# A four-layer graph network: the attention rows stay in two PSUM banks, and the other six are split anew

## The chip, the cores and the metric

The kernel runs on one core of a Trainium2 chip. The metric is the device time in microseconds of one execution. The figure before is the median of three executions. Everything is float32. The profile of one more execution gives the start and length of every instruction on the engines: TensorE (PE; its weight loads are PEld), VectorE (DVE), ScalarE (ACT) and GpSimd (POOL).

## The reference, cut to what matters

Input x holds 128 graphs of 128 nodes with 512 features; adj is one 128x128 matrix. Four layers follow each other, each with a residual and a layer norm:

```python
def layer0(x):  return einsum('bnd,do->bno', einsum('nm,bmd->bnd', adj, x), weight) + bias
def layer1(x):                                   # scores without softmax, normed by row
    q, k, v = x @ Wq.T, x @ Wk.T, x @ Wv.T
    rel = adj.T * einsum('bnd,bmd->bnm', q, k)
    return einsum('bnm,bmd->bnd', rel / norm(rel, axis=2, keepdims=True), v)
def layer2(x):                                   # attention from two dot products per node
    h = x @ W
    s1, s2 = h @ a[:512, 0], h @ a[512:, 0]
    e = leaky_relu(s1[:, :, None] + s2[:, None, :], 0.2) * adj
    return elu(einsum('bij,bjf->bif', softmax(e, axis=2), h) + beta * h)
def layer3(x):                                   # C - A is the bias: both use adj
    A = einsum('od,bdn->bon', adj, x); C = A + b
    return max(relu(A[:, :, None, :] + (C - A)[:, :, :, None]), axis=-1)
for layer in (layer0, layer1, layer2, layer3):
    x = layernorm(x + layer(x))
```

Since h = x W, the two dot products per node are x · (W a1) and x · (W a2): two rows of 512 numbers that are the same for every node and graph. The kernel computes them once and calls them wa.

## The kernel before

Graphs go in 32 groups of four. Work is emitted in pieces, each with a place in a table; all pieces are sorted by place, and every engine runs its own in that order. A group is spread over some 110 places and a new one begins every 28, so pieces of several groups stand among each other. The three dense products with 512x512 weights, and the q-k product with a merged matrix m_qk, are done by seven block products in place of eight (a Strassen scheme), in three PSUM regions r0, r1 and r2.

```python
psum = tile_pool(name="psum", bufs=4, space=PSUM)        # 4 buffers of each tag
def bank(name):                                          # one bank of 128 x 512 fp32
    return psum.tile([P, D], FP, tag="ps", name=name)
...
wa = const.tile([P, 2, D], FP)                           # SBUF
...
def prepare_rows():                                      # once
    for i in range(2):
        p = bank(f"p_wa{i}")
        for k in range(K):                               # K = 4
            pe.transpose(p[:, k * P : (k + 1) * P],
                         col[:, i, k : k + 1].to_broadcast([P, P]), ident)
        act.copy(wa[:, i, :], p)
    dve.tensor_reduce(wa_sum, wa, AX.X, ALU.add, negate=True)
...
ORDER = (1, 2, 6, 5, 7, 3, 4)                            # of the seven products
REGION = {1: 0, 6: 0, 7: 0, 4: 0, 2: 1, 5: 2, 3: 2}      # the region each adds to
def product(at, name, mul, s, w, c, fresh, begin=None):
    def step(i):
        where = REGION[i]
        first = i in (1, 2, 5)
        if first:
            r[where] = psum.tile([P, 2, H], FP, tag="r", name=f"r{where}_{name}")
        mul(r[where], s["f"][i], bw[w][i], first)        # 4 matmuls of 256 columns
    def out(i):                                          # the region as it stands, to a block
        p, dst = r[REGION[i]], c(*BLOCK[i])
        if fresh and i in (1, 6, 5, 4):
            act.copy(dst, p)
        else:
            dve.tensor_tensor(dst, p, dst, ALU.add)
    for n, i in enumerate(ORDER):
        emit(at[n], step, i)
        emit(at[n] + 0.72, out, i)
```

Products are named by their use: r_y for layer 0 (added to x), r_m and r_v for layer 1 (to tT and v), r_z for layer 2 (to c). The pieces of layers 1 and 2 around the dots:

```python
def attend(b):                                           # p_o
    s["o", b] = bank(f"p_o1_{g}_{b}")
    pe.matmul(s["o", b], s["relT"]..., s["v"][:, b, :], start=True, stop=True)
def residual(b):
    dve.scalar_tensor_tensor(x2[g][:, b, :], s["o", b], s["rn"][:, b : b + 1],
                             x1[g][:, b, :], op0=ALU.mult, op1=ALU.add)
    stats(s, f"1_{g}", b, x2[g][:, b, :])                # bn_stats, bn_aggr
def dots(b):
    for i in range(2):
        scr = work.tile([P, D], FP, tag="scr", bufs=2, ...)
        dve.scalar_tensor_tensor(scr, x2[g][:, b, :], 1.0, wa[:, i, :],
                                 op0=ALU.mult, op1=ALU.mult,
                                 accum_out=s["d"][:, i, b : b + 1])
def scale_dots():                                        # three small operations on d
    ...
# norm: ve = var + eps (VectorE), rstd = ve ** -0.5 (GpSimd), then the apply (ScalarE)
def spread():                                            # p_s: d to all partitions
    ... pe.transpose(...)
def direct(b):                                           # last group only, in place of r_z
    s["c", b] = psum.tile([P, D], FP, tag="r", name=f"c_{g}_{b}")
    for k in range(K):
        pe.matmul(s["c", b], s["zT"][:, k, ...], w2_sb[:, k, :], start=(k == 0), stop=(k == K - 1))
def elu(b):                                              # x<-c,x and x<-m,x
    dve.scalar_tensor_tensor(x, s["c", b], 0.0, x2[g][:, b, :], op0=ALU.max, op1=ALU.add)
    dve.scalar_tensor_tensor(x, s["m", b], 1.0, x, op0=ALU.min, op1=ALU.add)
```

GpSimd meanwhile adds the bias of layer 0 (x<-x,bias_sb) and forms the sums that the block products need (s_y, s_x, s_z), all from SBUF. Part of the table:

```python
residual=row(51.0, 1), dots=row(54.2, 1.1), norm1=[55.2], scale=[58.8],
```

where row(a, step) is four places, one for each graph.

Of the kernel before, what the change touches and what calls it, by code (L numbers as in the profile page):

```python
# [8 lines left out]
FP = mybir.dt.float32  # L9
# [20 lines left out]
def kernel(  # L30
# [33 lines left out]
    pe, dve, act, pool = (InOrder(tc, e) for e in (nc.tensor, nc.vector, nc.scalar, nc.gpsimd))  # L64
    sync = InOrder(tc, nc.sync)
    B, N, D = x.shape
    P = 128
# [3 lines left out]
    H = D // 2  # L71
# [4 lines left out]
    const = ctx.enter_context(tc.tile_pool(name="const", bufs=1))  # L76
    data = ctx.enter_context(tc.tile_pool(name="data", bufs=2))
    work = ctx.enter_context(tc.tile_pool(name="work", bufs=1))
    small = ctx.enter_context(tc.tile_pool(name="small", bufs=4))
    psum = ctx.enter_context(tc.tile_pool(name="psum", bufs=4, space=bass.MemoryType.PSUM))  # L80

    def bank(name):
        return psum.tile([P, D], FP, tag="ps", name=name)

    def on_all(row, n):

# [37 lines left out]
    ident = const.tile([P, P], FP)  # L124
# [3 lines left out]

    adjT = const.tile([P, P], FP)
    pt = bank("p_adjT")  # L130
    pe.transpose(pt[:, :P], adj_sb, ident)
    act.copy(adjT, pt[:, :P])
# [2 lines left out]

    m_qk = const.tile([P, K, D], FP)
    wvT = const.tile([P, K, D], FP)
    wa = const.tile([P, 2, D], FP)
    wa_sum = const.tile([P, 2], FP)
    beta_i = const.tile([P, P], FP)  # L140
    beta_b = beta_i[:, None, :].to_broadcast([P, G, P])
# [21 lines left out]
    def prepare_qk(c):  # L163

        pm = bank(f"p_m{c}")
        for e in range(K):
            pe.matmul(
                pm,
                wq_sb[:, e, c * P : (c + 1) * P],
                wk_sb[:, e, :],  # L170
                start=(e == 0),
                stop=(e == K - 1),
            )
        act.copy(m_qk[:, c, :], pm)
        if c == K - 1:
            bw["m"] = weight_blocks(m_qk, "m")

    def prepare_v(c):
        pv = bank(f"p_wv{c}")
        for e in range(K):  # L180
            pe.transpose(pv[:, e * P : (e + 1) * P], wv_sb[:, e, c * P : (c + 1) * P], ident)
        act.copy(wvT[:, c, :], pv)
        if c == K - 1:
            bw["v"] = weight_blocks(wvT, "v")

    col = const.tile([P, 2, K], FP)
# [15 lines left out]
    def prepare_rows():  # L202

        for i in range(2):
            p = bank(f"p_wa{i}")
            for k in range(K):
                pe.transpose(
                    p[:, k * P : (k + 1) * P], col[:, i, k : k + 1].to_broadcast([P, P]), ident
                )
            act.copy(wa[:, i, :], p)  # L210
        dve.tensor_reduce(wa_sum, wa, AX.X, ALU.add, negate=True)
        dve.tensor_scalar(beta_i, ident, beta_sb, None, op0=ALU.mult)

# [6 lines left out]
    def emit(at, f, *args):  # L220
        pieces.append((at, lambda: f(*args)))
# [5 lines left out]
    def row(at, step, n=G):  # L227
        return [at + i * step for i in range(n)]
# [6 lines left out]
        move=row(20.5, 0.1), x_sums=row(25.3, 0.5), m=row(28, 1, 7), scores=row(36.5, 1),  # L235
        masked=[39.95], squares=[40.4], turn_rel=[40.3],
        move_rel=row(41.2, 0.1), inverse=[42.5], v=row(42, 1, 7), attend=row(50.6, 1),
        residual=row(51.0, 1), dots=row(54.2, 1.1), norm1=[55.2], scale=[58.8],
        apply1=row(65.4, 0.33),
        spread=[61.6], leaky=[62.0], weighted=[63.4], greatest=[64.3], exps=[64.4],  # L240
        divide=[65.8], turn_att=[68.6], with_beta=[69.0], gather=row(71.5, 1),
# [15 lines left out]
            scale=[5.6], apply1=row(24.3, 0.8), spread=[6.9], leaky=[7.4], weighted=[9.0],  # L257
# [11 lines left out]
            scale=[47.0], apply1=row(47.5, 0.8), spread=[48.9], leaky=[49.4], weighted=[51.0],  # L269
# [69 lines left out]
    def product(at, name, mul, s, w, c, fresh, begin=None):  # L339


        r = {}

        def step(i):
            if i == 1 and begin is not None:
                begin()
            where = REGION[i]
            first = i in (1, 2, 5)
            if first:
                r[where] = psum.tile([P, 2, H], FP, tag="r", name=f"r{where}_{name}")  # L350
            mul(r[where], s["f"][i], bw[w][i], first)

        def out(i):
# [9 lines that stand above are left out]
# [251 lines left out]
    def layer2(g, t):  # L614
        s = {}
# [83 lines left out]

        def direct(b):  # L700

            s["c", b] = psum.tile([P, D], FP, tag="r", name=f"c_{g}_{b}")
            for k in range(K):
                pe.matmul(
                    s["c", b],
                    s["zT"][:, k, b * P : (b + 1) * P],
                    w2_sb[:, k, :],
                    start=(k == 0),
                    stop=(k == K - 1),
                )  # L710
# [25 lines left out]
        if g < NG - 1:  # L736
            left_factors(t["z_sums"], s, "zT", "s_yz", f"z_{g}", 0)
            product(t["z_w"], f"z_{g}", by_rows, s, "2", rows_of(lambda: s["c"]), True, begin)
        else:
            each(t["z_w"], direct)  # L740
# [35 lines left out]
    each(row(18.0, 0.1), prepare_v)  # L776
    each(row(29.2, 1.8), prepare_dots)
    emit(40.7, prepare_rows)
    emit(61.0, prepare_2)
    for g in range(NG):  # L780
# [33 lines left out]
```

## Time and profile before

| | |
|---|---|
| device time, median of 3 | 2239.06 us (2235.84 to 2239.59) |
| profiled execution | 2236.61 us, of which the span from first to last instruction is 2234.4 us |
| granted TensorE clock | 0.996 of full speed in the mean |
| DMA | 115.15 MB, 52 GB/s in the mean; queues' share of the engines 20% |

In the profile's lines an instruction stands by the tile that it writes and those that it reads (out<-in), with buffer and group numbers left out: scr<-x,wa is a dot, r_m<-xT,m_qk a block product of m, tT<-r_m the addition that reads its region, x<-p_o,rn,x the residual of layer 1, p_s the spread of the dots' result d. A line "A <- B: us, times, longest" says how long in total engine and tile A waited for B. In a timeline each line is a start in us, a length in us, and the instruction (x8: eight in a row); the bracket at its end is the idle time of the engine before it and what ended it. Each float32 matmul of the program appears as two records, so that a block product of four matmuls is "x8". The chain that ended last is 75% TensorE and 20% VectorE.

### The profile page before, as it was taken

How to read it: one execution, taken by the hardware profiler on the slowest of the kernel's cores; microseconds unless marked ns; L12 is line 12 of the kernel's file. 1: busy time of each engine (PE TensorE's matmuls, PEld its weight loads, DVE VectorE, ACT ScalarE, POOL GpSimd, SP SyncE). 2: the span in 40 equal slices, each digit the busy share in tenths (PEclk: the TensorE clock that was granted, in tenths of full speed). 3: DMA queues.
4: the chain of work that ended last, by engine and by line, in shares of the span. 5: the costliest groups of instructions: out<-in, count | busy, mean ns of one | idle time of the engine just before them, and what ended most of it. 6: DMA issues, size and time to landing. Idle time of an engine off the chain costs nothing.

```text
span 2234.4 us, 31661 instructions
## 1 busy us (share of the span) xinstructions
PE 2182.9 (98%) x11073; PEld 1842.1 (82%) x11073; DVE 1794.9 (80%) x3534; ACT 980.0 (44%) x1936; POOL 983.1 (44%) x743
## 2 busy tenths in 40 slices
PE   7999999999999999999999999999999999999996
PEld 5888888888888888888888888888888888888873
DVE  4668888778878788888788888788888788887788
ACT  2224444444444454444444444444344444444535
POOL 3435454435455344544344554344553354443322
PEclk9999999999999999999999999999999999999998
DMA  4010222211222211222201222202222112221101
GB/s 166 25 32 19 60 57 62 62 28 40 60 59 62 62 19 48 59 60 62 59 19 52 58 61 62 52 22 55 57 62 63 41 28 59 58 62 43 21 28 57
DMA packets 333294, 115.15 MB, mean 52 GB/s; under 512 B 297424, under 2 KB 297552, under 8 KB 333136
## 3 DMA queue, kind: packets, MB, share of 16 engines
q1 hardware_dynamic: 331936, 110.77, 19.6%
q10 hardware_dynamic: 1200, 2.36, 0.3%
q8 instruction: 89, 1.46, 0.3%
q14 instruction: 69, 0.57, 0.1%
HBM read 39.65 MB, written 33.55 MB: 33 GB/s over the span
## 4 chain that ended last, share of the span: by engine, by line
PE 75%; DVE 20%; issue 3%; POOL 1%; ACT 1%; DMA 0%; DVEq 0%; ACTq 0%; POOLq 0%
PE r_v L26 17%; PE r_y L26 15%; PE r_z L26 14%; PE r_m L26 8%; DVE scr L26 6%; DVE x L26 6%; PE p_z L26 5%; PE p_o L26 5%; PE p_a L26 5%; PE p_rel L26 4%; DVE st L26 2%; PE p_y L26 2%; DVE tT L26 1%; DVE d L26 1%; PE p_m L26 1%
## 5 line engine op out<-in xcount | busy, mean ns | idle before, releaser
L26 ACT ACTIVATE x<-x,nmean,rstd 128x512 f32<-128x512 f32 x512 | 385.8, 808 | 187.5 <-DVE nmean L26 187.4
L26 DVE BATCH_NORM_STATS2 st<-x 128x6 f32<-128x512 f32 x512 | 352.1, 688 | 56.7 <-ACT x L26 47.9
L26 DVE SCALAR_TENSOR_TENSOR scr<-x,wa 128x512 f32<-128x512 f32 x256 | 286.2, 1169 | 0.0
L26 POOL TENSOR_TENSOR rstd<-ve,mhalf 128x4 f32<-128x4 f32 (+1 forms) x134 | 145.2, 1083 | 286.9 <-DVE ve L26 280.7
L26 POOL TENSOR_TENSOR x<-x,bias_sb 128x512 f32<-128x512 f32 x128 | 193.2, 1519 | 76.9 <-PE p_y L26 76.4
L26 POOL TENSOR_TENSOR s_x<-xT 128x512 f32<-128x512 f32 x64 | 95.8, 1497 | 256.5 <-DMA xT<-xB 237.6
L26 ACT ACTIVATE x<-x,top 128x512 f32<-128x512 f32 x128 | 92.4, 722 | 229.1 <-DVE top L26 228.8
L26 DVE TENSOR_TENSOR x<-r_y,x 128x512 f32<-128x512 f32 x224 | 151.4, 676 | 27.1 <-PE r_y L26 27.0
L26 ACT COPY c<-r_z 128x512 f32<-128x512 f32 x124 | 71.8, 579 | 221.5 <-PE r_z L26 221.5
L26 ACT COPY yT<-p_y 128x512 f32<-128x512 f32 x128 | 75.1, 587 | 206.5 <-PE p_y L26 206.5
L26 PEld LDWEIGHTS p_y<-adjT,x 128*128 128x128 f32 x1024 | 135.8, 195 | 13.1 <-ACT adjT L26 5.2
L26 DVE SCALAR_TENSOR_TENSOR x<-p_o,rn,x 128x512 f32<-128x512 f32 x128 | 95.9, 749 | 59.9 <-PE p_o L26 56.0
L26 PE MATMUL p_y<-adjT,x 128*128 128x128 f32 x1024 | 136.7, 278 | 6.4 <-ACT adjT L26 4.9
L26 PEld LDWEIGHTS p_z<-eT,x 128*128 128x128 f32 x1024 | 133.9, 192 | 8.4 <-DVE x L26 1.2
L26 DVE SCALAR_TENSOR_TENSOR x<-m,x 128x512 f32<-128x512 f32 x128 | 129.7, 1013 | 13.6 <-DVE x L26 0.9
L26 PEld LDWEIGHTS p_rel<-xT,tT 128*128 128x128 f32 x1024 | 134.1, 191 | 7.4 <-DVE tT L26 0.8
L26 POOL TENSOR_TENSOR s_z<-zT 128x512 f32<-128x512 f32 x31 | 39.3, 1267 | 224.0 <-ACT zT L26 224.0
L26 PE MATMUL p_rel<-xT,tT 128*128 128x128 f32 x1024 | 134.9, 275 | 0.6 <-DVE tT L26 0.6
L26 PE MATMUL p_z<-eT,x 128*128 128x128 f32 x1024 | 134.8, 275 | 0.4 <-DVE x L26 0.4
L26 PE MATMUL p_a<-x,adjT 128*128 128x512 f32 x256 | 131.2, 597 | 3.6 <-ACT x L26 1.9
L26 ACT COPY tT<-r_m 128x512 f32<-128x512 f32 x128 | 75.7, 591 | 132.9 <-PE r_m L26 132.9
L26 PE MATMUL p_o<-v,relT 128*128 128x512 f32 x256 | 130.3, 593 | 0.0
(119 smaller groups left out, 5008.6 us busy)
## 6 DMA issues: line engine op xcount, KB each, us to landing
out_dram<-x SPq DMA_DIRECT2D x128, 256.0 KB, 2.5
x<-in_x_dram SPq DMA_DIRECT2D x31, 1024.0 KB, 5.8
xT<-xB SPq DMA_DIRECT2D x480, 64.0 KB, 2.3
relT<-relB SPq DMA_DIRECT2D x512, 16.0 KB, 1.8
w_sb<-in_L_gnn_weight_dram ACTq DMA_DIRECT2D x1, 1024.0 KB, 5.9
x<-in_x_dram SPq DMA_DIRECT2D x4, 256.0 KB, 7.9
wq_sb<-in_L_gnn_Wq_dram SPq DMA_DIRECT2D x1, 1024.0 KB, 12.1
wk_sb<-in_L_gnn_Wk_dram SPq DMA_DIRECT2D x1, 1024.0 KB, 14.9
```

Source lines behind the costliest of these rows:

```text
L26: return lambda *args, **kw: self.tc.keep_in_program_order(op(*args, **kw))
```

## The change

Each row of wa is first transposed on TensorE into a PSUM bank, from where ScalarE copies it to SBUF. The change leaves the rows in PSUM, in a tile of two banks that lives to the end, and the dots read them there. That is meant to take one of a dot's two inputs out of SBUF. Six banks remain: the general tag "ps" has 3 in place of 4, and the tag "r" (4) becomes "r0" with 2 for region 0 and the last group's direct products, and "r12" with 1 for regions 1 and 2 together. The table moves the dots between the residuals, and norm1 and scale forward.

```diff
-    psum = ctx.enter_context(tc.tile_pool(name="psum", bufs=4, space=bass.MemoryType.PSUM))
+    psum = ctx.enter_context(tc.tile_pool(name="psum", bufs=1, space=bass.MemoryType.PSUM))
     def bank(name):
-        return psum.tile([P, D], FP, tag="ps", name=name)
+        return psum.tile([P, D], FP, tag="ps", name=name, bufs=3)
@@
-    wa = const.tile([P, 2, D], FP)
+    wa = psum.tile([P, 2, D], FP, tag="wa", name="wa")
@@ prepare_rows
         for i in range(2):
-            p = bank(f"p_wa{i}")
             for k in range(K):
                 pe.transpose(
-                    p[:, k * P : (k + 1) * P], col[:, i, k : k + 1].to_broadcast([P, P]), ident
-                )
-            act.copy(wa[:, i, :], p)
+                    wa[:, i, k * P : (k + 1) * P],
+                    col[:, i, k : k + 1].to_broadcast([P, P]),
+                    ident,
+                )
@@ TABLE
-        residual=row(51.0, 1), dots=row(54.2, 1.1), norm1=[55.2], scale=[58.8],
+        residual=row(51.0, 1), dots=[51.7, 53.8, 54.9, 55.6], norm1=[54.6], scale=[57.2],
@@ product, step
-                r[where] = psum.tile([P, 2, H], FP, tag="r", name=f"r{where}_{name}")
+                r[where] = psum.tile(
+                    [P, 2, H],
+                    FP,
+                    tag="r0" if where == 0 else "r12",
+                    name=f"r{where}_{name}",
+                    bufs=2 if where == 0 else 1,
+                )
@@ direct
-            s["c", b] = psum.tile([P, D], FP, tag="r", name=f"c_{g}_{b}")
+            s["c", b] = psum.tile([P, D], FP, tag="r0", name=f"c_{g}_{b}", bufs=2)
```

## The prediction

> **What bounds the kernel now.** I read the page's busy times first, then TensorE's own waits, then the timeline of one group (the kernel runs 32 groups of four graphs; from about 220 us to 2130 us they look alike).
>
> The page, parts 1 and 5 (busy us and share; then group, count, busy us, mean ns, idle before):
>
> ```profile
> PE 2182.9 (98%) x11073; PEld 1842.1 (82%) x11073; DVE 1794.9 (80%) x3534; ACT 980.0 (44%) x1936; POOL 983.1 (44%) x743
> ...
> L26 DVE SCALAR_TENSOR_TENSOR scr<-x,wa 128x512 f32<-128x512 f32 x256 | 286.2, 1169 | 0.0
> ...
> L26 DVE SCALAR_TENSOR_TENSOR x<-p_o,rn,x 128x512 f32<-128x512 f32 x128 | 95.9, 749 | 59.9 <-PE p_o L26 56.0
> ...
> L26 DVE SCALAR_TENSOR_TENSOR x<-m,x 128x512 f32<-128x512 f32 x128 | 129.7, 1013 | 13.6 <-DVE x L26 0.9
> ```
>
> TensorE is the bound. How much of its 2183 us is really lost I worked out from the starts of its matmuls: from one start to the next it takes 216 ns for 256 columns, 429 ns for 512, 112 ns for 128 (109 ns for a transpose) when nothing holds it. Those, summed over all 11,073, give 2161.5 us. The first starts at 3.4 us, and about 13.6 us pass after the last start at 2220.8. What the starts lose beyond this is 56.4 us: 20.8 before 220 us (loads and preparation), 19.6 from 220 to 2130, and 16.0 after 2130. So a change to VectorE can win a part of 56 us, 2.5% of the time, and never the sum of its own savings.
>
> The three operations shown have 128x512 elements each. The dots (scr<-x,wa) take 1169 ns in the mean, the residual, which has one input in PSUM, 749. The means of the first and third hide two kinds: of the single records of the dots the shortest tenth is at 679 ns and the longest tenth at 1748 to 1755, with little between; those of the residual all lie from 718 to 754.
>
> TensorE's waits (us in total, times, longest):
>
> ```profile
> PE r_m L26 <- DVE tT L26: 6.8, 5, 1.7
> ...
> PE r_y L26 <- DVE x L26: 4.4, 17, 0.4
> ...
> PE p_s L26 <- DVE d L26: 3.1, 2, 2.1
> ```
>
> All three are TensorE waiting for VectorE just behind the dots: an addition that must read a PSUM region before the next product adds to it, and the transposes of the dots' result. By the starts, the losses in front of r_y and of r_m are the 19.6 us of the steady part almost wholly: 0.6 to 1.0 us before r_y in about half of the groups, and 1.4 us before r_m in four, with some tenths before the next r_y product.
>
> One group, timeline (start, us, engine): VectorE, then GpSimd, then TensorE.
>
> ```profile
> 1050.80 0.68 DVE L26 SCALAR_TENSOR_TENSOR scr<-x,wa 128x512 f32<-128x512 f32 x1
> ...
> 1051.42 0.68 DVE L26 SCALAR_TENSOR_TENSOR scr<-x,wa 128x512 f32<-128x512 f32 x1
> ...
> 1052.03 1.74 DVE L26 SCALAR_TENSOR_TENSOR scr<-x,wa 128x512 f32<-128x512 f32 x1
> ...
> 1053.70 1.75 DVE L26 SCALAR_TENSOR_TENSOR scr<-x,wa 128x512 f32<-128x512 f32 x1
> ...
> 1055.38 0.68 DVE L26 TENSOR_TENSOR tT<-r_m,tT 128x512 f32<-128x512 f32 x1
> ```
> ```profile
> 1050.28 1.46 POOL L26 TENSOR_TENSOR rstd<-ve,mhalf 128x4 f32<-128x4 f32 x1
> 1051.72 4.86 POOL L26 TENSOR_TENSOR x<-x,bias_sb 128x512 f32<-128x512 f32 x3
> ```
> ```profile
> 1048.94 1.89 PE L26 MATMUL r_m<-xT,m_qk 128*128 128x256 f32 x8
> ...
> 1054.18 1.89 PE L26 MATMUL r_m<-s_x,m_qk 128*128 128x256 f32 x8
> ...
> 1060.25 0.60 PE L26 MATMUL p_s<-ident,d 128*128 128x128 f32 x4
> 1062.13 1.99 PE L26 MATMUL r_m<-xT,t_m 128*128 128x256 f32 x8 [1.28 <-DVE tT L26]
> 1063.96 3.62 PE L26 MATMUL r_y<-w_sb,yT 128*128 128x256 f32 x16
> ```
>
> Two dots run in 0.68 us; the two that begin while GpSimd adds the bias take 1.74 us, a GpSimd operation longer. The r_m block at 1048.94 ends at about 1050.8, but its reader, the addition at 1055.38, stands behind the dots. The lateness runs on to the bracketed stall of 1.28 us.
>
> **What the Trainium skill says.** "SBUF — State Buffer", Who interferes with whom: a VectorE instruction with two SBUF inputs contends with a GpSimd instruction that reads SBUF, and one with at most one SBUF input does not; the shared pair is an exclusive lock, so the loser waits for the whole instruction. The trace agrees: 0.68 against 1.74 us for the two-SBUF dots, never over 0.754 us for the residual with its PSUM input, whatever GpSimd does. "PSUM — Partial Sum Buffer", Specifications (TRN2): eight banks of 2 KiB per partition, and a VectorE instruction may take one tensor input from PSUM. So both broadcast rows (2 x 512 fp32) are exactly two banks, and six stay for everything else; no run yet shows what six do. "Perfetto Trace Analysis", Identifying the Most-Contended Engine: TensorE's busy share is a poor measure of its headroom. The trace agrees: busy 2182.9 us, of which 2161.5 are pitch.
>
> **The change, part by part.**
>
> *The dots read PSUM.* 256 dots lose their second SBUF input. A quiet two-SBUF dot takes 0.68, the PSUM residual 0.75; I take 0.70. VectorE saves 256 x (1.169 - 0.70) = 120 us, 3.75 us a group. GpSimd also waited for the dots (1.50 to 1.79 us for operations that take 1.27 when alone); perhaps 50 us of its 983 go. Neither sum is on the path.
>
> *The dots stand earlier.* In the built program the first pair comes after the first residual, the second after the third, and the rstd power is asked for before the last two pairs; the three small d operations come before the r_m addition. Walking one group with TensorE's starts above and 0.70 per dot: last residual's statistics at about 1046.0, the r_z addition at 1046.2 to 1046.9, four dots to 1049.7, d (rstd ready at about 1049.6) to 1050.6, then the r_m addition at 1050.9 to 1051.6, now held by TensorE itself, in place of 1055.38 to 1056.06. The later additions keep some 2 us of this. The p_s wait and both r stalls go.
>
> *Two copies of wa by ScalarE* (1.1 us, once) go. Nothing.
>
> *PSUM split anew.* Before: 4 banks for ps, 4 for the r regions and the last group's direct c. After: ps 3, r0 and c 2, r1 and r2 together 1. For each PSUM tile I took from the trace its first matmul's start less the end of the last read of the tile it will now follow. In the steady groups: ps with 3 banks keeps at least 4.2 us of slack; r0 with 2 keeps 15. The single r1/r2 bank is the tight one: r1_v, r2_v, r1_z, r2_z have 2.4 to 4.3 us, r2_y 0.8, r1_m 0.5, but r1_y -0.3 and r2_m -1.1 in the median (negative means a wait). With the old dots this would cost 1.4 us a group. But the readers behind the negative ones are those very additions behind the dots: in the walk r2_m (wanted at 1054.2) finds its bank read at 1051.6, r1_m (1048.9) at 1046.9, r1_y (about 1064.3 without the stall) at 1062 to 1063.8 even if all four ELU operations in front collide with GpSimd. So no new wait in the steady groups.
>
> Start: p_wv with 3 banks waits 2.1 us for a copy, of which the next tile's old position gives back 1.6: -0.5. In group 0 the r2_m product must wait for the r_m addition (-5.1 us with old dots; about 2.7 with new), while the 2.2 us p_s stall behind it goes: -0.5. Group 1's 2.4 us go: +2.4. Sum: +1.4.
>
> End: TensorE's waits for d and tT at 2137 and 2144 (1.1 + 0.8) go. Then p_o and p_z with 3 banks wait up to 2.9 us for residuals (about 2.0 net), and the third direct c waits 1.9 for the first one's ELU, with 2 banks. The last dots save only two collisions, 2.1 us. I put the end at +2, plus or minus 3.
>
> Sum: 19.6 (say 19.5) + 1.4 + 2 = 23 us; 2239 - 23 = 2216.
>
> **Rivals.**
> *The single r1/r2 bank becomes the new wait.* For: two negative slacks of eight, and the thin walk of r1_y. Against: both are in the shadow of the dots. If it costs 1 us a group the gain is eaten: some 2240; with 1.4 us more and the old stalls kept, 19.6 + 39, so 2278.
> *VectorE's saving comes back as other collisions.* The ELU operations (x<-m,x, 1013 ns) move under the bias additions in place of the s_y sums; for: VectorE is 80% busy and GpSimd's total shrinks little. If half of the 3.75 us a group comes back, most r_y stalls stay: 2225 to 2230.
> *The end decides.* It is bound by VectorE's chain; two banks for c and three for p_z could cost 3 us more than I count: 2221.
>
> **Range and chances.** The steady gain cannot exceed 19.6, and start and end lose at most about 5 more than counted: 2207 to 2230 should hold it 8 times in 10. A gain of 2% would be 44.8 us, four fifths of all that TensorE loses; a loss of 2% needs the first rival at its worst. So within 2% is nearly certain.
>
> **What would show it.** Dots at 0.68 to 0.75 us without a second kind; VectorE busy about 1675 us, GpSimd below 960; PE <- DVE tT and DVE d gone from TensorE's waits, r_m or r_y starts without gaps, group after group 66.8 us apart. Wrong if TensorE's loss in the steady part stays above 8 us, or if r2_m or r1_y wait for VectorE's additions in most groups; or if p_z, c and p_a lose over 5 us at the end.

## The result, and the profile after

The changed kernel takes 2219.39 us (median of four executions, 2218.65 to 2220.8); the kernel before, run beside it, 2239.21 us (2235.84 to 2239.59). The ratio is 0.9916, 95% interval 0.9898 to 0.9933: 0.8% faster. The prediction was 2216 us.

The page of the changed kernel: busy times (part 1), the chain that ended last (part 4), and three groups of part 5 (count, busy us, mean ns, idle before).

```profile
PE 2173.1 (98%) x11073; PEld 1841.6 (83%) x11073; DVE 1652.0 (74%) x3534; ACT 979.0 (44%) x1934; POOL 908.2 (41%) x743
...
PE 94%; DVE 3%; POOL 1%; ACT 1%; issue 0%; DMA 0%; ACTq 0%; DVEq 0%; POOLq 0%
...
L26 POOL TENSOR_TENSOR x<-x,bias_sb 128x512 f32<-128x512 f32 x128 | 171.2, 1340 | 137.8 <-PE p_y L26 137.2
L26 DVE SCALAR_TENSOR_TENSOR x<-m,x 128x512 f32<-128x512 f32 x128 | 114.4, 894 | 112.7 <-ACT m L26 102.4
...
L26 DVE SCALAR_TENSOR_TENSOR scr<-x,wa 128x512 f32<-128x512 f32 x256 | 161.4, 675 | 0.0
```

VectorE does 142.9 us less and GpSimd 74.9 us less, and the time falls by 20. That is what a bound of TensorE looks like: its own line stays at 98%, and the chain, which was 75% TensorE and 20% VectorE, is now 94% TensorE. The dots are down to 675 ns in the mean. GpSimd's bias additions, which stood beside them, went from 1519 to 1340 ns, and the ELU operations x<-m,x from 1013 to 894.

One steady group of the changed kernel on VectorE (start us, length us):

```profile
1042.60 0.67 DVE L26 SCALAR_TENSOR_TENSOR scr<-x,wa 128x512 f32<-128x512 f32 x1
...
1044.41 0.68 DVE L26 SCALAR_TENSOR_TENSOR scr<-x,wa 128x512 f32<-128x512 f32 x1
...
1045.02 0.94 DVE L26 SCALAR_TENSOR_TENSOR d<-mv,wa_sum,d 128x4 f32<-128x4 f32 x2
1046.07 0.17 DVE L26 TENSOR_TENSOR d<-d,rstd 128x8 f32<-128x8 f32 x1
1046.29 0.69 DVE L26 TENSOR_TENSOR tT<-r_m,tT 128x512 f32<-128x512 f32 x1
```

and on TensorE:

```profile
1049.53 1.89 PE L26 MATMUL r_m<-s_x,m_qk 128*128 128x256 f32 x8
...
1055.61 0.60 PE L26 MATMUL p_s<-ident,d 128*128 128x128 f32 x4
1056.05 1.89 PE L26 MATMUL r_m<-xT,t_m 128*128 128x256 f32 x8
```

No dot takes 1.7 us any more. The addition at 1046.29 ends at 1046.98, and the product that must follow it in the single r12 bank starts at 1049.53: 2.5 us of slack. Of the kernel before, the same addition started 1.2 us *after* the start of that product. None of the three TensorE lines has a bracket, so none waited; the r_m stall of 1.28 us that the kernel before had there is gone.

What TensorE still waits for in the changed kernel (us in total, times, longest):

```profile
PE p_a L26 <- DVE mx L26: 4.9, 2, 3.2
...
PE r_m L26 <- DVE tT L26: 4.4, 1, 4.4
...
PE p_wv L26 <- ACT wvT L26: 1.9, 1, 1.9
PE c L26 <- DVE x L26: 1.8, 1, 1.8
PE r_y L26 <- DVE tT L26: 1.5, 1, 1.5
```

Each of these happens once or twice, in the start or at the end; none belongs to a steady group.

I counted TensorE's loss beyond pitch as in the prediction, here with places in the program instead of times: *start* until the first r0 product of m in group 3, *steady* until that of group 31, *end* after it. The last column is the time from that product of group 31 to the end of the span; at the end it says more than the loss, since the chain runs through VectorE too there. A steady loss of -1.7 means none: the median pitches overstate a little. Each ratio is taken to executions of the kernel before beside that run; these had medians of 2235.8 to 2239.2 us, so that the ratios compare better than the times.

| kernel | us (median) | ratio, 95% interval | start | steady | end | us after |
|---|---|---|---|---|---|---|
| before | 2239.2 | 1 | 20.8 | 19.6 | 16.0 | 105.5 |
| the change: rows in PSUM, split, new places | 2219.4 | 0.9898 to 0.9933 | 23.8 | -1.7 | 19.6 | 106.9 |
| split alone | 2264.1 | 1.0104 to 1.0139 | 27.1 | 37.5 | 22.0 | 108.8 |
| new places alone | 2215.5 | 0.9888 to 0.9926 | 16.0 | 4.2 | 14.3 | 103.8 |
| split and new places, rows in SBUF | 2280.2 | 1.0173 to 1.0218 | 26.7 | 53.6 | 20.0 | 106.9 |
| rows in PSUM and split, old places | 2212.3 | 0.9877 to 0.991 | 17.5 | -1.7 | 18.0 | 105.3 |
| the same, free banks used at the end | 2212.3 | 0.9878 to 0.9907 | 18.4 | -1.7 | 15.9 | 105.8 |
| the change, group 0's scale later | 2211.9 | 0.9876 to 0.9906 | 17.7 | -1.7 | 18.1 | 105.4 |
| before, without the bias addition | 2206.8 | 0.9851 to 0.9884 | 12.5 | -1.7 | 15.9 | 105.3 |
| PSUM, old places, start and end mended | 2210.0 | 0.9866 to 0.9895 | 15.6 | -1.7 | 15.9 | 105.8 |
| PSUM, old places, start mended alone | 2210.4 | 0.9861 to 0.9894 | 15.5 | -1.7 | 18.5 | 105.3 |

The profiled spans differ by 2234.4 - 2217.6 = 16.8 us, and the table accounts for them: +21.3 in the steady part, -3.0 at the start, -1.4 after group 31's product. The medians differ by 3 us more because the profiled execution of before was 2.6 us quicker than its median.

### The profile page after: what moved, and what is told of

Same layout as the page of the kernel before. It is cut to its first block, busy times and chain, and to the rows that moved or that the text cites. A ratio compares the mean times of both kernels' runs of the same rounds, so it can differ in the third digit from the quotient of the medians.

```text
span 2217.6 us, 31631 instructions
## 1 busy us (share of the span) xinstructions
PE 2173.1 (98%) x11073; PEld 1841.6 (83%) x11073; DVE 1652.0 (74%) x3534; ACT 979.0 (44%) x1934; POOL 908.2 (41%) x743
## 3 DMA queue, kind: packets, MB, share of 16 engines
q10 hardware_dynamic: 1200, 2.36, 0.3%
## 4 chain that ended last, share of the span: by engine, by line
PE 94%; DVE 3%; POOL 1%; ACT 1%; issue 0%; DMA 0%; ACTq 0%; DVEq 0%; POOLq 0%
PE r_y L26 17%; PE r_m L26 17%; PE r_v L26 17%; PE r_z L26 17%; PE p_z L26 5%; PE p_rel L26 5%; PE p_y L26 5%; PE p_o L26 5%; PE p_a L26 5%; DVE st L26 1%; DVE x L26 1%; PE p_eT L26 1%; PE p_m L26 1%; PE p_s L26 1%; ACT x L26 1%; POOL x L26 1%
## 5 line engine op out<-in xcount | busy, mean ns | idle before, releaser
L26 POOL TENSOR_TENSOR rstd<-ve,mhalf 128x4 f32<-128x4 f32 (+1 forms) x134 | 132.2, 986 | 307.1 <-DVE ve L26 300.8
L26 POOL TENSOR_TENSOR x<-x,bias_sb 128x512 f32<-128x512 f32 x128 | 171.2, 1340 | 137.8 <-PE p_y L26 137.2
L26 DVE SCALAR_TENSOR_TENSOR x<-m,x 128x512 f32<-128x512 f32 x128 | 114.4, 894 | 112.7 <-ACT m L26 102.4
L26 POOL TENSOR_TENSOR s_x<-xT 128x512 f32<-128x512 f32 x64 | 82.2, 1285 | 254.2 <-DMA xT<-xB 243.3
L26 DVE SCALAR_TENSOR_TENSOR scr<-x,wa 128x512 f32<-128x512 f32 x256 | 161.4, 675 | 0.0
L26 PE MATMUL r_m<-s_x,m_qk 128*128 128x256 f32 x512 | 123.1, 384 | 4.4 <-DVE tT L26 4.4
```

The costliest lines, as they stand in the source:

```text
L26: return lambda *args, **kw: self.tc.keep_in_program_order(op(*args, **kw))
```

## The experiments

My theory after the result was that the steady stalls were the late r_m additions, that the quick dots cleared them, and that the new places mattered little. The rivals were that the split costs what the negative slacks say, and that the earlier places do the work. Rows in PSUM without the new split would need ten banks of the eight, so every version with the rows in PSUM has the split.

### The new split alone

The rows of wa stay in SBUF and the dots where they were; only the banks are divided as in the change (ps 3, r0 2, r12 1; two banks stay unused).

```diff
-    psum = ...tile_pool(name="psum", bufs=4, ...)
+    psum = ...tile_pool(name="psum", bufs=1, ...)
-        return psum.tile([P, D], FP, tag="ps", name=name)
+        return psum.tile([P, D], FP, tag="ps", name=name, bufs=3)
-                r[where] = psum.tile([P, 2, H], FP, tag="r", ...)
+                r[where] = psum.tile([P, 2, H], FP, tag="r0" if where == 0 else "r12", ...,
+                                     bufs=2 if where == 0 else 1)
-            s["c", b] = psum.tile([P, D], FP, tag="r", ...)
+            s["c", b] = psum.tile([P, D], FP, tag="r0", ..., bufs=2)
```

> The kernel before with the new PSUM split alone (rows of wa in SBUF, two banks left empty, old table). Theory A, waits overlap: a TensorE that is held at r_m is not held again at r_y, so each steady group loses about the 1.1 us of r_m in place of the 0.7 us it lost before; with some 7 us more at start and end: 2250 to 2260 us. Rival of the prediction, waits add: 1.4 us a group come on top of the old ones: 2278 us. Rival B, the split is free away from start and end: 2245 us.

Measured: 2264.1 us, ratio 1.0122 (1.0104 to 1.0139). TensorE's waits, the first line:

```profile
PE r_m L26 <- DVE tT L26: 36.2, 31, 4.8
```

Once in nearly every group; without the one of 4.8 us at the start, 1.05 us in the mean. So the negative slack of -1.1 us read from the kernel before was real and cost what it said. But the steady loss is 37.5 us, 17.9 more than before, and not 39 more: a wait for the r_m addition puts the r_y products behind it later too, so that the old stalls there vanish in it. Waits on one chain overlap; the prediction's figure of 2278 us for its first rival had added them.

### The new places alone

```diff
-        residual=row(51.0, 1), dots=row(54.2, 1.1), norm1=[55.2], scale=[58.8],
+        residual=row(51.0, 1), dots=[51.7, 53.8, 54.9, 55.6], norm1=[54.6], scale=[57.2],
```

> The kernel before with the new places of dots, norm1 and scale alone (rows in SBUF, 4 + 4 banks). Theory P, the PSUM rows are what wins: dots still collide, less than half of the steady gain: 2229 us or more. Rival T, the places alone suffice: the first two pairs of dots now run in VectorE's idle time between residuals, before GpSimd's sums begin, so the lateness behind the dots falls by some 2.3 of 4.4 us, the steady waits go (19.6 us and the negative rest), and nothing is paid at start and end: 2214 to 2219 us, as fast as the changed kernel or faster.

Measured: 2215.5 us, ratio 0.9907 (0.9888 to 0.9926), no less of a gain than the whole change, with dots that still take 1141 ns in the mean and VectorE busy for 1791.5 us. What is left of the stalls:

```profile
PE r_y L26 <- DVE x L26: 2.8, 7, 1.3
```

So a gain of this size can be had without the PSUM rows. What matters is when the additions behind the dots run, and with four banks for the regions the table alone does nearly all of that.

### Split and new places, rows in SBUF

Both edits above together, that is, the change without its PSUM rows.

> The changed kernel with the rows back in SBUF (new split, new places). Theory P: the single r1/r2 bank needs the quick dots, so r_m waits come back in most groups: 2235 to 2250 us. Rival T: the places leave about 0.4 us of slack at r_m, so steady groups stay clean and only start and end cost: 2219 to 2226 us.

Measured: 2280.2 us, ratio 1.0195 (1.0173 to 1.0218). Both expectations fell: places that help with the old banks hurt with the new ones. VectorE in one group of this kernel:

```profile
1135.84 1.77 DVE L26 SCALAR_TENSOR_TENSOR scr<-x,wa 128x512 f32<-128x512 f32 x1
...
1137.54 1.75 DVE L26 SCALAR_TENSOR_TENSOR scr<-x,wa 128x512 f32<-128x512 f32 x1
...
1139.22 1.75 DVE L26 SCALAR_TENSOR_TENSOR scr<-x,wa 128x512 f32<-128x512 f32 x1
...
1140.90 0.34 DVE L26 SCALAR_TENSOR_TENSOR d<-mv,wa_sum,d 128x4 f32<-128x4 f32 x2
1141.35 1.05 DVE L26 TENSOR_TENSOR d<-d,rstd 128x8 f32<-128x8 f32 x1
1142.32 0.68 DVE L26 TENSOR_TENSOR tT<-r_m,tT 128x512 f32<-128x512 f32 x1
```

and TensorE:

```profile
1139.93 1.05 PE L26 MATMUL p_y<-adjT,x 128*128 128x128 f32 x8
1143.05 3.44 PE L26 MATMUL r_m<-s_x,m_qk 128*128 128x256 f32 x8 [2.06 <-DVE tT L26]
```

In the new order the d operations stand ahead of the r_m addition. Three collided dots and 1.4 us of d operations are between the addition and the end of its product, and the r_m product behind it now waits 2.06 us, then runs 3.44 us instead of 1.89 (the last section returns to this). The waits of r_m for tT sum to 44.0 us in 31 times.

### Rows in PSUM and split, old places

The change without its edit of the table.

```diff
-        residual=row(51.0, 1), dots=[51.7, 53.8, 54.9, 55.6], norm1=[54.6], scale=[57.2],
+        residual=row(51.0, 1), dots=row(54.2, 1.1), norm1=[55.2], scale=[58.8],
```

> The changed kernel with the old places of dots, norm1 and scale (rows in PSUM, new split). If quick dots alone suffice, the eight dots take some 5 us in a row after the last residual, the r_m addition ends at about the same moment as in the changed kernel, and the time is the same within 3 us: 2217 to 2223 us. If places and PSUM rows each bring half, about 2229 us.

Measured: 2212.3 us, ratio 0.9894 (0.9877 to 0.991). This kernel has nothing left in its steady groups, like the change, and loses 17.5 us at the start instead of 23.8. The head of TensorE's waits:

```profile
PE p_y L26 <- ACT adjT L26: 5.1, 1, 5.1
PE p_a L26 <- DVE mx L26: 4.9, 2, 3.2
...
PE p_wv L26 <- ACT wvT L26: 1.9, 1, 1.9
PE c L26 <- DVE x L26: 1.8, 1, 1.8
PE r_y L26 <- DVE tT L26: 1.5, 1, 1.5
```

It is the list of the change but for r_m <- tT, which falls from 4.4 to 0.6 us. With quick dots the tight bank is free in time in either order, so the new places win nothing, and they cost 7.9 us by the profiled spans (5 by the ratios). The time is better than expected: I hadn't thought that these places could do harm.

### The start: group 0's scale later

The change's only long wait for an r_m addition lies at the start: by the table, group 1's product waits for an addition that stands behind group 0's d operations. On VectorE:

```profile
108.64 0.68 DVE L26 SCALAR_TENSOR_TENSOR scr<-x,wa 128x512 f32<-128x512 f32 x1
...
109.25 2.46 DVE L26 SCALAR_TENSOR_TENSOR d<-mv,wa_sum,d 128x4 f32<-128x4 f32 x2
111.81 1.12 DVE L26 TENSOR_TENSOR d<-d,rstd 128x8 f32<-128x8 f32 x1
112.86 0.68 DVE L26 TENSOR_TENSOR tT<-r_m,tT 128x512 f32<-128x512 f32 x1
```

GpSimd:

```profile
109.21 3.70 POOL L26 TENSOR_TENSOR x<-x,bias_sb 128x512 f32<-128x512 f32 x3
```

and TensorE:

```profile
108.14 1.05 PE L26 MATMUL p_y<-adjT,x 128*128 128x128 f32 x8
113.59 3.78 PE L26 MATMUL r_m<-s_x,m_qk 128*128 128x256 f32 x8 [4.39 <-DVE tT L26]
```

The three d operations, with 4 or 8 elements per partition, hold VectorE for 3.6 us in front of the addition, while GpSimd makes three bias additions of 1.2 us each. The edit gives group 0 alone a later place for them, behind the addition.

```diff
-    FIRST = {0: dict(turn=row(20.4, 0.3)), ...}
+    FIRST = {0: dict(turn=row(20.4, 0.3), scale=[58.0]), ...}
```

> The changed kernel with one place changed: group 0's three small d operations stand behind its first r_m addition. Theory D: these three, which took 1.24, 1.30 and 1.12 us beside GpSimd's bias additions, are what holds the r2_m product 4.6 us at the start; that wait falls to about 1 us and the time to 2214 to 2217 us. Rival: group 0 is late by the dots between its residuals and the third ps bank; the wait stays above 3 us and the time at 2218 to 2220 us.

Measured: 2211.9 us, ratio 0.9891 (0.9876 to 0.9906): 7.5 us off the change by the medians (5.6 by the ratios), where 2 to 5 had been expected. The same product on TensorE:

```profile
109.59 1.99 PE L26 MATMUL r_m<-s_x,m_qk 128*128 128x256 f32 x8 [0.79 <-DVE tT L26]
```

The wait falls by 3.6 us and the product's length from 3.78 to 1.99 us: behind the long wait it had run at half clock. The start's loss of 17.7 us is that of the old places (17.5), and so is the time. So the place of three operations of group 0 makes the whole difference between the new places and the old: 6.1 us at the start, and 1.5 at the end, where a stretch of half clock is gone (below).

### The end: free banks used there

On rows in PSUM with the old places: the last group's later direct products c take the two wa banks, free by then, as one tile, and one p_o, one p_z (of group 30) and two p_a take r12 and r0 banks where these are idle.

```diff
+            elif b == 2:
+                late = psum.tile([P, 2, D], FP, tag="wa", name=f"c_{g}_late")
+                s["c", 2], s["c", 3] = late[:, 0, :], late[:, 1, :]
@@ p_o (group 31, b 3) and p_a (group 31, b 3): tag "r0"; p_z (group 30, b 2) and p_a (group 31, b 1): tag "r12"
```

> Rows in PSUM, new split, old places, and in the last two groups banks that have come free are used: the third and fourth direct c lie in the two banks of the rows (their dots are done), and one p_o, one p_z and two p_a tiles in banks of the r regions. Theory A, the bank waits at the end count: TensorE waits of 2.0 us before c, 1.8 and 3.4 us before p_a and about 1 us before p_z shrink and the time falls by 2 to 4 us against rows, split and old places: 2208 to 2210 us. Theory B, the end is VectorE's chain and these waits lie beside it: no more than 1 us: 2211 to 2213 us.

Measured: 2212.3 us, ratio 0.9893 (0.9878 to 0.9907), the same as without it. TensorE's waits changed as meant: c <- x is gone, p_a <- mx falls from 4.9 to 1.4 us, and this line takes its place.

```profile
PE p_a L26 <- ACT x L26: 2.9, 2, 1.4
```

The end's loss falls by 2.1 us and the time after group 31's product does not (105.3, 105.8). That doesn't show that the bank waits cost nothing, for the edit brought two delays of its own. The two late products share one tile, c_late, and ScalarE's read of the first starts only when both are done, though the first is done halfway. TensorE, ScalarE and VectorE there:

```profile
2178.68 7.03 PE L26 MATMUL c_late<-w_sb,zT 128*128 128x512 f32 x16
...
2185.81 0.60 ACT L26 ACTIVATE m<-c_late 128x512 f32<-128x512 f32 x1 [2.05 <-PE c_late L26]
...
2186.44 0.69 DVE L26 SCALAR_TENSOR_TENSOR x<-c_late,x 128x512 f32<-128x512 f32 x1 [2.34 <-ACT m L26]
```

And a stretch of half clock at 2167 us, which the same version without these banks doesn't have, holds the first direct product for 4.46 us in place of 3.60. What the banks are worth with two separate tiles was not tried.

### Start and end mended, and the start alone

The last p_wv tile goes to the r12 bank, which is free then, and the t_2 sums on VectorE (1.64 us each, which stood in front of an r_m addition) move one and a half places back. Once on top of the end's banks, once without them.

```diff
-        pv = bank(f"p_wv{c}")
+        pv = psum.tile([P, D], FP, tag="r12", name=f"p_wv{c}", bufs=1) if c == K - 1 else bank(f"p_wv{c}")
-    emit(61.0, prepare_2)
+    emit(62.5, prepare_2)
```

> As the run with the banks at the end, and at the start one p_wv tile lies in the r1/r2 bank, and the preparation of layer 2's weight sums comes behind the r_m addition that it held up. If waits before p_wv (2.1 us) and r1_y (1.6 us) count in full the time falls by 3 to 4 us against that run, if they lie beside other waits by 1 or less; all in all 2205 to 2212 us, the fastest of all.

> The rows in PSUM with the split and the old places, and the two mends of the start alone: the last p_wv tile in the r12 bank, the t_2 sums of prepare_2 one and a half places later; the end as in the change. Theory S (the start mends are worth 2 to 3 us and the end's banks nothing): 2209 to 2211, the start's loss 15 to 16, like the version with start and end mended (2210.0). Rival: the two mends only work together, or 2210.0 was scatter: 2212 or more.

Measured: 2210.0 us (ratio 0.9881, 0.9866 to 0.9895) and 2210.4 us (0.9878, 0.9861 to 0.9894). The first falls between its two expectations; the start's loss drops by 2.8 us against the version with the end's banks. The second has nearly the same time with the end as in the change, so the two lines at the start are enough. Their own gain over the old places without them is small: the start's loss falls from 17.5 to 15.5 us in the profiled executions, while the intervals of the two ratios overlap. Both beat the kernel before and the change. They compute all of it, and the simpler one is the second: the change with its table edit undone and these two lines. The new places alone, with the old banks and a mended start, were not tried.

### Before, without the bias addition

The kernel before with the 128 bias additions of layer 0 left out, so that its output lacks the bias. It takes one of the dots' two main collision partners away and leaves rows, banks and places as they were.

```diff
-        each(t["bias"], biased)
```

> The kernel before (rows in SBUF, 4 + 4 banks, old places) without the addition of layer 0's bias, which GpSimd does beside the dots; its output lacks that bias. Theory L, a dot is long because it waits for one GpSimd operation: of 256 dots 129 are long, 60 of them under the bias; those 60 take 0.68 us, the rest stay, the mean falls from 1169 to 900 to 960 ns, and the waits of the steady groups go: 2214 to 2222 us. Rival, the long kind is a cost of two SBUF inputs that GpSimd has no part in: the mean stays above 1100 ns.

The dots, from the groups by shape (busy us, mean ns):

```profile
L26 DVE SCALAR_TENSOR_TENSOR scr<-x,wa 128x512 f32<-128x512 f32 x256 | 223.9, 925 | 0.0
```

Of the 256 dots of the kernel before 129 were long ones: 60 under the bias addition, 67 under the s_x sums, 2 under s_z. Taking 60 of them from 1.75 to 0.68 us gives 1169 - 60 x 1070/256 = 918 ns; 925 was measured, within the expected 900 to 960. With only half of the collisions gone the steady loss is already -1.7. The time, 2206.8 us, is below what was expected, because the start lost 8.3 us less as well; I put that down to the bias additions missing from the first layer's own chain there, which no run tells apart. It is no fair rival of the others, as it leaves work out.

## Why the prediction was right, and where it was not

**The bound and the steady part: right.** That TensorE's 56 us of loss are the ceiling, and that 19.6 of them lie in the steady part, was read from the pitch. The steady part gave back 21.3 us against 19.5 predicted, so groups start 66.8 us apart as expected ((2110.7 - 239.9)/28).

**The dots: right, and a little quick.** 675 ns against the 700 I took, with no second kind. The Trainium skill says in "SBUF — State Buffer", Who interferes with whom, that a VectorE instruction with two SBUF inputs contends with a GpSimd instruction that reads SBUF, and the case agrees twice: with one input in PSUM every dot took about 0.68 us, and with GpSimd's bias addition absent the dots from SBUF fell to 925 ns. VectorE saved 142.9 us where I predicted 120: the dots 124.8, and 34.2 that I hadn't counted in the ELU operations (x<-c,x from 864 to 716 ns, x<-m,x from 1013 to 894), less 10.7 for the d<-mv,wa_sum,d operations and 5.7 for ve<-mv. GpSimd saved 74.9, not some 50.

**The single r1/r2 bank: right.** The r_m addition still stands behind dots, but behind quick ones, and that was what counted. In the changed kernel r2_m has 1.7 to 2.6 us of slack in the steady groups, r1_m 1.5 to 2.1, r1_y 0.85. The first rival was well founded (the split alone costs 1.2%), but it needed slow dots. Its figure of 2278 us was wrong, as it added waits that overlap.

**The second rival fell.** I had the ELU operations moving into more collisions; they had fewer.

**What I gave the table edit was wrong.** The prediction credited the dots' new places and the earlier d operations with clearing the stalls together with PSUM. The runs show that PSUM with the split clears the steady part without the places (-1.7 us), that the places nearly do so without PSUM and with the old banks (4.2 us), and that together with PSUM and the split they only cost.

**The start: predicted +1.4, measured -3.0.** The failed term is "In group 0 the r2_m product must wait for the r_m addition (... about 2.7 with new)". By the table that product is group 1's, behind group 0's dots. It waited 4.56 us by the starts, and the products behind it lost 2.15 us more at half clock. The wait was mis-sized by the three d operations: the prediction's walk of a steady group gives them 0.9 us, and at the start they took 2.46 and 1.12, each beside a bias addition. I had asked of each large operation what GpSimd does beside it, and not of the small ones. The means over the whole run don't show this, since the d operations meet GpSimd in the steady groups in either order (d<-mv,wa_sum,d 618 ns in the change and 348 with the old places, d<-d,rstd 197 and 808). It is their place at the start that counts.

The term of p_wv held: it lost 2.09 us, and the 1.68 us that TensorE lost there before (p_y, waiting for wvT) are gone. Two other losses were not foreseen: an r_m addition behind the t_2 sums, 1.63 us, and 1.7 us in the products behind a stretch of half clock at 56.6 us.

**The end: predicted +2, measured -1.4.** The waits I named came: c 1.98 us, p_o and p_z 1.06, 0.84 and 0.6, and p_a's two of 1.84 and 3.37, which I hadn't sized and which make p_a alone pass my mark of 5 us for the end. But their sum is not the cost: the version with the old places has the same waits, and its time after group 31's product is 105.3 us against 105.5 before. In their place others went, such as p_a's 1.92 and 1.59 and p_s's 1.14; the 0.8 us before p_rel, which were to go, stayed. The -1.4 of the change is a stretch of half clock at 2173 us, behind which the products lost 1.6 us. The two versions with the end's banks have such a stretch too, at 2167 and 2163 us, and the old places without them, with or without the start mended, don't. Whether one occurs may depend on where the fixed stretches of the last section fall; that was not tried.

So 19.5 + 1.4 + 2 = 23 became 21.3 - 3.0 - 1.4 = 17 in the spans, and 19.8 in the medians. The nearness of 2216 to 2219 owes something to that difference of medians and spans.

## What to carry to other kernels

Where TensorE bounds, sum its losses beyond pitch by stage first: that is the ceiling, and a saving of 143 us on VectorE was worth the 21 us that its late additions cost. An operand that is read often and never changes is taken out of the lock with GpSimd by leaving it in PSUM, but count the banks: the split by itself cost 1.2%, and only the quick dots made it free. When a change does several things, run each alone and each left out; here the places were worth as much as the whole change, and in company with the PSUM rows they cost 5 to 8 us.

## What the hardware showed beyond that

Long TensorE waits cost more than their length: behind some of them the granted clock is 0.5 for 3.41 us or twice that. I first took it for a limit on a wait's length. Two runs tested this on the version with rows in PSUM and old places, which loses nothing in the steady groups. In groups 4 to 28 VectorE gets extra dots, whose results are thrown away, ahead of the addition on which r2_m waits; their sum differs by group, in shuffled order.

```diff
         def out(i):
+            if i == 2 and name[0] == "m" and int(name[2:]) in DELAY:
+                for n, width in enumerate(DELAY[g]):
+                    dve.scalar_tensor_tensor(scr[:, :width], x1[g][:, 0, :width], 1.0, wa[:, 0, :width],
+                                             op0=ALU.mult, op1=ALU.mult, accum_out=acc)
```

> The rows in PSUM with the split and the old places (2212 us), where TensorE loses nothing in the steady groups. In each of groups 4 to 28 VectorE gets extra dots (their result is thrown away) just ahead of the addition that reads region r1 of the m product, 3.0 to 5.4 us of them in all, in shuffled order, so that the r2_m product waits a planned 0.9 to 3.5 us once a group (its slack was 1.7 to 2.6). Theory W (a long wait halves the granted clock afterwards): no stretch of halved clock behind waits under 1.5 us, one of 3.4 us behind most waits over 2.3 us, whatever the group's number, each costing some 1.7 us more; with about 25 waits of 2.2 us in the mean (55 us) and a dozen stretches (20 us) the time is 2275 to 2300. Rival R (the halved stretches of the other runs stood behind waits by chance, or belong to the start and the end): no halved clock between 220 and 2130 us, and 2260 to 2270.

The waits came out shorter than planned, 2.7 us at most, and the time (of one execution, as in the next run) at 2238.0 us, below both ranges. There was one halved stretch in the steady part, behind the wait of 2.70 us, and none behind those of 2.52, 2.14, 2.11 and 2.00. That speaks against the rival, and is too little for a rule. So the delays were lengthened:

```diff
-        us = 3.0 + 0.1 * k
+        us = 4.6 + 0.12 * k
```

> As the run with 3.0 to 5.4 us of extra dots ahead of the r1_m addition in groups 4 to 28, but with 4.6 to 7.5 us of them, so that the r2_m waits are a planned 2.2 to 5 us. There one stretch of halved clock stood behind the longest wait (2.70 us) and none behind one of 2.52, of 2.14 or of 2.11 us. Theory W2 (the clock is judged by fixed stretches of 3.41 us, and halved for the next one when most of a stretch lay idle): behind waits of 2.2 to 3 us about half get a halved stretch, behind waits over 4 us all do; each costs up to 1.7 us. Rival L (a plain limit on the wait's length, some 2.6 us): none below 2.5 us, all above 2.7. Time 2275 to 2320.

Measured: 2307.0 us, with waits of 1.0 to 4.6 us that sum to 65.4 us and a steady loss of 93.8. Thirteen waits had a halved stretch behind them. Among them is one of 2.33 us, while of two waits of 2.61 and 2.62 us one had it and the other not. The plain limit falls. TensorE around two waits of nearly the same length (2.36 and 2.33 us by the starts):

```profile
309.06 1.99 PE L26 MATMUL r_m<-s_x,m_qk 128*128 128x256 f32 x8 [2.20 <-DVE tT L26]
...
587.25 2.60 PE L26 MATMUL r_m<-s_x,m_qk 128*128 128x256 f32 x8 [2.17 <-DVE tT L26]
```

Every halved stretch of one trace starts at the same remainder when its time is divided by 3.4133 us (in this trace, and in the nine others that have more than one). So I cut each trace into such stretches. The stretches around the two waits (columns: from and to in us, length, busy us of TensorE, its weight loads, VectorE, ScalarE and GpSimd, then the granted clock, the DMA share and GB/s):

```profile
305.20:308.60 3.40, 1.67 (x12) 1.40 (x10) 3.40 (x13) 1.60 (x3) 1.67 (x2) 1.00 0.00 0
308.60:312.00 3.40, 2.94 (x17) 2.71 (x18) 3.07 (x8) 0.01 (x1) 0.00 (x0) 1.00 0.00 0
...
585.10:588.50 3.40, 1.25 (x6) 1.12 (x7) 3.22 (x11) 1.60 (x3) 1.27 (x1) 1.00 0.00 0
588.50:591.90 3.40, 3.40 (x14) 3.05 (x13) 1.57 (x3) 0.30 (x1) 0.26 (x1) 0.50 0.00 0
```

The second wait lies whole in one stretch and leaves 1.25 us of work in it; the first is shared with the next, and leaves 1.67. Over all thirteen traces, from 90 us to the last drop of the clock, of the stretches at full clock with an idle time of 0.5 to 2.03 us (some 270, by the starts) none was followed by a halved one; of the 46 with more, 43 were, and the three exceptions had 2.05, 2.09 and 2.10 us. The limit is thus near 60% of a stretch. In the changed kernel it is what the wait at 109 us shows:

```profile
107.80:111.20 3.40, 1.39 (x11) 1.15 (x9) 3.40 (x8) 1.07 (x2) 3.40 (x4) 1.00 0.77 290
111.20:118.00 6.80, 4.41 (x12) 3.70 (x13) 2.23 (x3) 0.00 (x0) 1.71 (x2) 0.50 0.00 0
```

A halved stretch costs about half of itself, by an estimate that puts all loss beyond the waits down to it: in the last run 93.8 + 1.7 - 65.4 = 30.1 us for 17 of them, 1.8 us each. The Trainium skill, in "TensorE: Matmul & The Clock Gate", Part 1: The HAM clock gate (the "warmup" mystery), says that activity is judged in a free-running window of 3413 ns, that the clock is halved after an idle one, and that gaps over some 3.4 us are to be avoided. The length and the fixed phase agree with these traces. The gap does not, and here the measurement decides: some 2.1 us of idle time in one window are enough, in one wait or in several. This also explains the split with the new places and rows in SBUF, where six waits of 2.2 to 2.5 us in the steady groups had a halved stretch behind them.
